# Cross attention and feed-forward: image units that make their weights once, turned by a trip through DRAM, and gate and up weights kept in DRAM

## The chip, the cores and the metric

The kernel runs on one core of one Trainium2 chip. The core has TensorE (matrix products; PE in the profile, with its weight loads as PEld), VectorE (DVE), ScalarE (ACT), GpSimd (POOL) and SyncE (SP), which here only issues transfers, and 16 DMA engines which all queues share. The metric is the device time of one execution in microseconds (us). Lower is better.

## The reference

Four batches of 1,024 tokens with 512 channels. Of each batch the first 768 tokens are image tokens, in three chunks of 256, and the last 256 are text.

```
q  = layernorm(x) @ Wq + bq                   # 16 heads of d = 32
k, v = ctx @ Wk + bk, ctx @ Wv + bv
s  = q k^T / sqrt(32), masked:                # an image query sees its own chunk of 256 keys
                                              # a text query sees 768 image keys and text keys up to its own
x  = x + softmax(s) v @ Wo + bo
y  = fake_quant(layernorm(x))                 # int8 steps, one scale for the whole tensor
h  = fake_quant(silu(y Wg^T) * (y Wu^T))      # 512 -> 1408, weights in int8 steps, one scale per row
x  = x + h Wd^T                               # 1408 -> 512
```

The softmax has to be that of the reference: the maximum of a row of scores is subtracted before the exponential. Only the kernel's inputs and this function count; how the weights of a softmax lie in memory on the way is free.

## The kernel before

**Units and steps.** The work of attention is cut into *blocks* of 256 queries (four per batch: three image blocks and the text block), a block into four groups of four heads, and a group into *parts*, the blocks of keys. An image block has one part (its own chunk), the text block four. One group and part is a *unit*: 256 queries, 256 keys, four heads. A batch has 12 image units and 16 text units, the whole attention 112; batches 0 to 2 are units 0 to 83, and batch 3 runs its first image block, then text, then the other two. One loop goes over the steps n, and step n holds pieces of several units:

- `maxima` of unit n: the scores with queries on partitions (TensorE, L446 image, L457 text; into two PSUM tiles of 128x1024, of which there are three pairs of banks for all scores), and from them on VectorE the negated maximum of each query (L450, L468). `minus_maxima` (L484, L485) splits it on GpSimd into two bf16 numbers in a tile nm2, and `shifts` (L492) has a DMA transpose turn that into rows, nmT.
- `weights` of unit n-5 (T_LAG): TensorE spreads the shift over the keys (L504), adds the scores *a second time*, now with keys on partitions (L509), and ScalarE takes the exponential into pT (L514, L518, 128x1024 each). GpSimd adds the two halves of keys into sp (L535).
- `values` of unit n-6 (V_LAG): TensorE multiplies pT by the values (L554) and, in the last part of a group, sums the weights with a matrix of ones (L573). ScalarE copies both out of PSUM (L964), VectorE takes the reciprocal of the sums (L588), and GpSimd multiplies (L589) into oT, from which the output product is made.

So an image unit computes its scores twice: the first for the maxima, the second the way round in which the value product needs the weights.

**What fills the rest.** Between these lie the projections of queries, keys and values and the output product (`column_groups`, L226: four products of 32 columns side by side), in "big" steps. `target(n)` says how many of them should be done by step n, `large(n)` takes one piece if the work is behind the target, and else an output. Projection results are taken by ScalarE (L295, L344), outputs by VectorE (L607), with the statistics of the second layer norm (L614 to L617). The inputs of a projection are loaded by `load_spread` (L142 to L146, four transfers of 128 KB on SP) and turned by a VectorE transpose in 32x32 blocks (`small_step`, L267). Behind the first batch's image units, `weight_unit` (L647 to L668) loads 128 rows of gate or up weights at a time, 22 in all, finds the scale on VectorE, rounds on ScalarE and GpSimd, and lets a DMA transpose (L668) put the result into wgT or wuT, which stay in SBUF until the feed-forward stage. Each block of x1_d, the residual in DRAM, is first filled with the bias (L883, SP's queue) and then gets x added (L885, GpSimd's queue).

**The order.** The program order is the order of issue on TensorE, VectorE, ScalarE and GpSimd; on SP, which carries most transfers, a scheduler sets it. An engine takes its instructions in order: one that waits holds all behind it.

**Feed-forward** starts after all attention: a reading of x1_d, rounding, gate and up products (`products`, L1116), SiLU (L1122), their product (L1143), rounding, and the down product (L1207, L1219).

## Time and profile before

| | us |
|---|---|
| median of the runs (three, 1126.51 to 1128.64) | 1127.62 |
| span of the profiled execution | 1126.9 |
| attention's first score product | 30.7 |
| batch 0: image units, text units | 97.3, 123.7 |
| batch 1: image units, text units | 90.5, 122.5 |
| batch 2: image units, text units | 89.1, 122.4 |
| batch 3 and the end of attention | 152.4 |
| feed-forward, from 828.6 | 298.3 |
| mean granted TensorE clock | 0.995 |
| moved by DMA: 135.87 MB, 121 GB/s over the span | |

A page of the profile gives the busy time of each engine over one execution, the span in 40 slices, the DMA queues, the chain of work that ended last (followed back from the last instruction), and groups of instructions: line, engine, operation, out<-in with partitions x elements, count, then busy time and the mean in ns of one, then the idle time of the engine just ahead of them and what ended it. Lines of a table by stage read: from and to, length, busy PE with its instructions, PEld, DVE, ACT, POOL, granted clock, mean DMA share, GB/s. In a list in order of time, a line is start, duration, engine, line, operation and count; successive instructions of one kind are drawn together.

In the fifth part of the page a reader finds the operations of `weights` and `values` of all 112 units: the second scores L509 with 113.8 us of TensorE, the exponentials L514 and L518 with 114.8 and 114.5 us of ScalarE, L535 with 189.3 and 140.2 us of GpSimd, the reciprocals L588 with 109.8 us of VectorE (63 of 1,743 ns).

### The profile page before, as it was taken

How to read it: one execution, taken by the hardware profiler on the slowest of the kernel's cores; microseconds unless marked ns; L12 is line 12 of the kernel's file. 1: busy time of each engine (PE TensorE's matmuls, PEld its weight loads, DVE VectorE, ACT ScalarE, POOL GpSimd, SP SyncE). 2: the span in 40 equal slices, each digit the busy share in tenths (PEclk: the TensorE clock that was granted, in tenths of full speed). 3: DMA queues.
4: the chain of work that ended last, by engine and by line, in shares of the span. 5: the costliest groups of instructions: out<-in, count | busy, mean ns of one | idle time of the engine just before them, and what ended most of it. 6: DMA issues, size and time to landing. Idle time of an engine off the chain costs nothing.

```text
span 1126.9 us, 31493 instructions
## 1 busy us (share of the span) xinstructions
PE 1106.6 (98%) x13829; PEld 553.9 (49%) x13851; DVE 783.9 (70%) x980; ACT 502.4 (45%) x701; POOL 532.0 (47%) x615
## 2 busy tenths in 40 slices
PE   9999999999999999999999999999999899998998
PEld 5545545454545444454545445555554344443344
DVE  2546677666576857666777657777667788877887
ACT  3234434353544334444434345545433465553553
POOL 1224546577755467775446467566752222110110
PEclk9999999999999999999999999999999899999999
DMA  7379645255744444332222113112321599310895
GB/s 234 101 219 284 114 96 127 61 113 98 121 62 115 93 105 78 101 81 63 59 84 80 48 60 83 47 51 63 114 67 58 179 295 255 70 38 23 302 386 194
DMA packets 138257, 135.87 MB, mean 121 GB/s; under 512 B 56060, under 2 KB 103432, under 8 KB 136712
## 3 DMA queue, kind: packets, MB, share of 16 engines
q1 hardware_dynamic: 115600, 91.91, 29.5%
q0 software_dynamic: 22208, 41.42, 14.3%
q8 instruction: 108, 1.77, 0.7%
q10 hardware_dynamic: 312, 0.53, 0.2%
q14 instruction: 29, 0.24, 0.1%
HBM read 79.96 MB, written 50.07 MB: 115 GB/s over the span
## 4 chain that ended last, share of the span: by engine, by line
PE 87%; POOL 4%; DVE 3%; ACT 2%; DMA 2%; issue 1%; SPq 0%; DVEq 0%; POOLq 0%; ACTq 0%
PE pv L226 10%; PE po L226 9%; PE av L554 9%; PE pp_q L226 8%; PE pp_kv L226 8%; PE t L509 7%; PE pg L1116 7%; PE pu L1116 7%; PE s L457 5%; PE pd L1219 5%; PE s L446 4%; POOL sp L535 3%; PE av L573 3%; PE t L504 3%; PE pd L1207 1%
## 5 line engine op out<-in xcount | busy, mean ns | idle before, releaser
L514 ACT ACTIVATE pT<-t 128x1024 f32<-128x1024 f32 x112 | 114.8, 1025 | 330.2 <-PE t L509 299.8
L535 POOL TENSOR_TENSOR sp<-sp,pT 128x1024 f32<-128x1024 f32 x84 | 189.3, 2254 | 43.2 <-ACT pT L518 39.8
L468 DVE TENSOR_REDUCE nmh<-s 128x2 f32<-128x1024 f32 (+1 forms) x128 | 145.2, 1157 | 61.2 <-PE s L457 59.0
L535 POOL TENSOR_TENSOR sp<-pT 128x1024 f32<-128x1024 f32 x59 | 140.2, 2375 | 95.7 <-ACT pT L518 87.3
L450 DVE TENSOR_REDUCE nmh<-s 128x4 f32<-128x1024 f32 x96 | 112.7, 1216 | 85.7 <-PE s L446 85.7
L226 PE MATMUL pp_q<-qT,Wq_sb 128*32 128x256 f32 x2048 | 121.3, 380 | 0.2
L226 PE MATMUL pv<-Wv_sb,kvT 128*32 128x512 f32 (+1 forms) x1088 | 120.5, 570 | 0.0
L554 PE MATMUL av<-pT,va 128*32 128x256 f32 (+1 forms) x1792 | 116.9, 377 | 0.0
L518 ACT ACTIVATE pT<-t 128x1024 f32<-128x1024 f32 x112 | 114.5, 1023 | 0.0
L509 PE MATMUL t<-qT,kT 32*128 32x256 f32 (+1 forms) x1792 | 113.8, 367 | 0.0
L226 PE MATMUL pp_kv<-kvT,Wk_sb 128*32 128x256 f32 x1920 | 112.5, 380 | 0.1
L226 PE MATMUL po<-Wo_sb,oT 128*32 128x512 f32 (+1 forms) x1120 | 112.1, 534 | 0.3
L588 DVE RECIPROCAL avs<-avs 128x256 f32<-128x256 f32 x63 | 109.8, 1743 | 0.0
L589 POOL TENSOR_TENSOR oT<-avs 128x256 f32<-128x256 f32 x63 | 48.0, 762 | 104.2 <-DVE avs L588 104.2
L509 PEld LDWEIGHTS t<-qT,kT 32*128 32x128 f32 x1792 | 88.3, 184 | 6.6
L1116 PE MATMUL pg<-xqT,wgT 128*128 128x512 bf16 x344 | 89.9, 381 | 1.1 <-DVE xqT L1077 0.5
L1116 PE MATMUL pu<-xqT,wuT 128*128 128x512 bf16 x345 | 89.8, 381 | 0.4
L1122 ACT ACTIVATE silu<-pg,sg 128x512 f32<-128x512 f32 x88 | 60.0, 686 | 64.9 <-PE pg L1116 62.8
L226 PEld LDWEIGHTS pp_q<-qT,Wq_sb 128*32 128x32 f32 x2048 | 63.3, 110 | 48.3 <-issue 5.8
L1143 DVE SCALAR_TENSOR_TENSOR h<-pu,su,silu 128x512 f32<-128x512 f32 x88 | 65.3, 746 | 30.3 <-PE pu L1116 27.6
L226 PEld LDWEIGHTS pp_kv<-kvT,Wk_sb 128*32 128x32 f32 x1920 | 60.2, 110 | 43.6 <-issue 2.3
L554 PEld LDWEIGHTS av<-pT,va 128*32 128x32 f32 x1792 | 47.0, 109 | 53.5 <-issue 30.3
(190 smaller groups left out, 1435.0 us busy)
## 6 DMA issues: line engine op xcount, KB each, us to landing
xt<-x_d SPq DMA_DIRECT2D x16, 1024.0 KB, 6.0
h<-h_d POOLq DMA_DIRECT2D x3, 2816.0 KB, 13.5
xb<-in_x_dram SPq DMA_DIRECT2D x16, 512.0 KB, 4.4
x_d<-bo_b SPq DMA_DIRECT2D x16, 512.0 KB, 5.7
x_d<-in_x_dram POOLq DMA_DIRECT2D x16, 512.0 KB, 7.6
xr<-x_d SPq DMA_DIRECT2D x16, 512.0 KB, 3.8
x_d<-xr POOLq DMA_DIRECT2D x16, 512.0 KB, 3.8
spread_kv<-in_ctx_dram SPq DMA_DIRECT2D x60, 128.0 KB, 3.0
```

What stands on the lines that cost most here:

```text
L226: nc.tensor.matmul(out[rows_of(j)], lhs[:, rows_of(j)], rhs, start=start, stop=stop, tile_position=(0, j * D), skip_group_check=True)
L450: nc.vector.tensor_reduce(nmh[:, h, :, :, 0], prs[h], AX.X, ALU.max, negate=True)
L468: nc.vector.tensor_reduce(nmh[:, h, :, i, half], s[:, :, :n], AX.X, ALU.max, negate=True)
L509: nc.tensor.matmul(prs[j // 2][:, j % 2, n, cols], kc[rows_of(j), g, n * P : (n + 1) * P], q[rows_of(j), g, cols], start=False, stop=(n == 1))
L514: nc.scalar.activation(pT[:, :2], prs[0], AF.Exp)
L518: nc.scalar.activation(pT[:, 2:], prs[1], AF.Exp)
L535: nc.gpsimd.tensor_tensor(sp[:, :, cols], a, pT[:, :, n, cols], ALU.add)
L554: nc.tensor.matmul(av[rows_of(j), 0, cols], va[:, n, g * P + j * D : g * P + (j + 1) * D], u.pT[:, j, n, cols], start=(u.part == 0 and n = ...
L588: nc.vector.reciprocal(avs[:, 1, :], avs[:, 1, :])
L1116: nc.tensor.matmul(ps, w[:, cc, ic * P : (ic + 1) * P], qT[:, cc, :], start=(cc == 0), stop=(cc == NCC - 1))
L1122: nc.scalar.activation(s, pg, AF.Silu, scale=sg[:, ic : ic + 1])
L1143: nc.vector.scalar_tensor_tensor(h[:, ic, :], pu, su[:, ic : ic + 1], s, ALU.mult, ALU.mult)
```

## The change

For the 36 image units of batches 0 to 2 (`u.rows`), the scores are made once, and the weights from them while queries are still on partitions:

- `exponents`: ScalarE reads the score tiles in PSUM, eight times 128x256 per unit, with the negated maximum as bias of each row, and sums each row as it goes (`accum_out`). The result is written in a blocked order (g n x k) into a tile E, a half unit (two heads) each; three buffers.
- `quotients`: VectorE takes the reciprocal of the 128x4 sums, GpSimd multiplies E by it (128x1024).
- `shuffle`: SP writes E to DRAM (512 KB; four buffers) and reads it back in four transfers of 128 KB into S (three buffers), so that blocks of 32 queries come to stand on the right partitions.
- `turned`: VectorE transposes S in 32x32 blocks into pT, keys on partitions.
- `row_values` at a lag of three steps (R_LAG): TensorE's value product, without the product for the sums; ScalarE copies the result straight into oT.

For these units `minus_maxima`, `shifts`, `weights` and `values` fall away. Inside a step the new pieces stand in this order: `maxima` of unit n, the `shuffle` of the second half of unit n-1, `turned` first half of unit n-2, `exponents` and `quotients` of the first half of unit n, the big step, the taking of its result, `exponents` of the second half, `turned` second half of unit n-2, the second `quotients`, the first half's `shuffle`; then what is left of text units in `weights` and `values`, and `row_values` of unit n-3. Batch 3 and all text units work as before.

Keys and values of image blocks are loaded with their rows in another order (`mixed`, eight transfers instead of four), to match the order of the keys in pT.

nmT has three buffers instead of five, nm2 three instead of four, and the gate and up weights no longer stay in SBUF beside these tiles: each transposed 128 rows go on to DRAM (`wq_d`, one more transfer on SP for each of 22), and `reload` brings both sets back (1.4 MB each) in batch 3, into the room of Wk, Wv and Wq, once the last projection and the last weight unit are done. The feed-forward products read them there.

The pacing changes too: in batches 1 to 3, `target` counts an image step in the first half of the image units three times, in the second half one and a half times, and a text step once; `large` no longer takes a piece ahead of the target in text steps; and an image step takes an output at its end if one waits and no other big step was taken there.

```diff
@@ -80,8 +80,7 @@
...
-    wgT = cpool.tile([P, NCC, FF], BF16, tag="wgT", name="wgT")
-    wuT = cpool.tile([P, NCC, FF], BF16, tag="wuT", name="wuT")
+    wq_d = {w: dram.tile([P, NIC, NCC * P], BF16, tag=f"wq_{w}_d", name=f"wq_{w}_d") for w in "gu"}
@@ -122,11 +121,13 @@
...
-        nmp = actx.enter_context(tc.tile_pool(name="nmp", bufs=5))
+        nmp = actx.enter_context(tc.tile_pool(name="nmp", bufs=3))
         qp = actx.enter_context(tc.tile_pool(name="qp", bufs=4))
         kp = actx.enter_context(tc.tile_pool(name="kp", bufs=7))
         ap = actx.enter_context(tc.tile_pool(name="ap", bufs=1))
-        wp = actx.enter_context(tc.tile_pool(name="wp", bufs=1))
+        bp = actx.enter_context(tc.tile_pool(name="bp", bufs=3))
+        wctx = ExitStack()
+        wp = wctx.enter_context(tc.tile_pool(name="wp", bufs=1, side="right"))
@@ -139,18 +140,29 @@
...
-        def load_spread(src, c):
...
             t = ld.tile([P, NQB * 2, P], F32, tag="cb", name=f"spread_{c}")
-            s = src.rearrange("(k q) (c m) -> c q k m", q=D, c=NCC)
             for i in range(NCC):
-                nc.sync.dma_start(t[i * D : (i + 1) * D], s[i])
+                to, cols = t[i * D : (i + 1) * D], slice(i * P, (i + 1) * P)
+                if not mixed:
+                    nc.sync.dma_start(to, src[:, cols].rearrange("(k q) m -> q k m", q=D))
+                    continue
+                for n in range(2):
+                    nc.sync.dma_start(to[:, n * 4 : (n + 1) * 4], src[:, cols].rearrange("(g n q) m -> n q g m", n=2, q=D)[n])
+            return t
...
@@ -441,6 +454,7 @@
...
             prs = [pair(f"s_{u.n}_{h}") for h in range(2)]
             if not k.text:
+                u.s, u.nmh = prs, nmh
@@ -467,6 +481,67 @@
...
+        def exponents(u, h):
+
+            e = bp.tile([P, 4, 2, 4, D], F32, tag="E", name=f"E_{u.n}_{h}")
+            sums = small.tile([P, 4], F32, tag="sums", name=f"sums_{u.n}_{h}", bufs=4)
+            for x in range(4):
+                jj, i = x // 2, x % 2
+                nc.scalar.activation(
+                    e[:, :, :, x, :].rearrange("p g n k -> p n g k"),
+                    u.s[h][:, jj, i, :].rearrange("p (n g k) -> p n g k", n=2, g=4),
+                    AF.Exp,
+                    bias=u.nmh[:, h, jj, i, 0:1],
+                    accum_out=sums[:, x : x + 1],
+                )
+            u.e[h], u.sums[h] = e, sums
+
+        def quotients(u, h):
+
+            nc.vector.reciprocal(u.sums[h], u.sums[h])
+            e = u.e[h].rearrange("p g n x k -> p (g n) x k")
+            nc.gpsimd.tensor_tensor(e, e, u.sums[h].unsqueeze(1).unsqueeze(3).to_broadcast([P, 8, 4, D]), ALU.mult)
+
+        def shuffle(u, h):
+
+            e = u.e.pop(h)
+            through = dram.tile([P, 4 * QB], F32, tag="e_d", name=f"e_d_{u.n}_{h}", bufs=4)
+            nc.sync.dma_start(through, e.rearrange("p g n x k -> p (g n x k)"))
+            u.spread[h] = t = bp.tile([P, 4, QB], F32, tag="S", name=f"S_{u.n}_{h}", bufs=3)
+            for g in range(4):
+                nc.sync.dma_start(t[g * D : (g + 1) * D], through.rearrange("(b q) (g f) -> g q b f", q=D, g=4)[g])
+
+        def turned(u, h):
+
+            if h == 0:
+                u.pT = wk2.tile([P, 4, 2, QB], F32, tag="pT", name=f"pT_{u.n}")
+            out = u.pT[:, 2 * h : 2 * h + 2].rearrange("p a b q -> p (a b q)").rearrange("p (y b k) -> p b y k", b=4, k=D)
+            nc.vector.transpose(out, u.spread.pop(h).rearrange("p b (y k) -> p b y k", k=D))
+
+        def row_values(u):
+
+            k, g = u.k, u.g
+            if "av" in state:
+                av = pair(f"av_{u.n}").rearrange("p a b q -> p (a b) q")[:, 0, :]
+            else:
+                av = ps_av.tile([P, 2, QB], F32, tag="av", name=f"av_{u.n}")[:, 0, :]
+            va = V[k.c]
+            pT = u.pT.rearrange("p a b q -> p (a b q)").rearrange("p (h n j q) -> p h n j q", h=2, n=2, j=2)
+            for n in range(2):
+                for j in range(4):
+                    nc.tensor.matmul(
+                        av[rows_of(j)],
+                        va[:, n, g * P + j * D : g * P + (j + 1) * D],
+                        pT[:, j // 2, n, j % 2, :],
+                        start=(n == 0),
+                        stop=(n == 1),
+                        tile_position=(0, j * D),
+                        skip_group_check=True,
+                    )
+            if g == 0:
+                k.begin()
+            return av
+
@@ -665,11 +742,13 @@
...
             def transpose():
-                nc.sync.dma_start_transpose(dst[:, :, ic * P : (ic + 1) * P], q)
+                t = wk2.tile([P, NCC, P], BF16, tag="wqT", name=f"wqT_{what}_{ic}", bufs=1)
+                nc.sync.dma_start_transpose(t, q)
+                nc.sync.dma_start(wq_d[what][:, ic, :], t.rearrange("p c f -> p (c f)"))
...
 
-        T_LAG, V_LAG = 5, 6
+        T_LAG, V_LAG, R_LAG = 5, 6, 3
@@ -680,6 +759,8 @@
...
+        for u in units[:LATE]:
+            u.rows, u.e, u.sums, u.spread = not u.k.text, {}, {}, {}
@@ -768,7 +849,9 @@
             first, n = 6 * BIG, n + 1.5
             if n < n_img:
                 return first + (NQB - 1) * first * n / n_img
-            return NQB * first * (1 + (n - n_img) / (n_img + n_text))
+            whole, n = divmod(n - n_img, n_img + n_text)
+            done = min(n, n_text) + 3 * min(max(n - n_text, 0), n_img / 2) + 1.5 * max(n - n_text - n_img / 2, 0)
+            return NQB * first * (1 + whole + done / (n_text + 4.5 * n_img / 2))
@@ -800,7 +883,7 @@
...
-                elif can_big(n) and spent < target(n) + 3 * BIG:
+                elif can_big(n) and spent < target(n) + (0 if units[n].k.text else 3 * BIG):
@@ -830,6 +913,15 @@
...
+        wT = {}
+
+        def reload(w):
+            if not wT:
+                wctx.close()
+                fw = ctx.enter_context(tc.tile_pool(name="fw", bufs=1, side="right"))
+                for x in "gu":
+                    wT[x] = fw.tile([P, NIC, NCC, P], BF16, tag=f"w{x}T", name=f"w{x}T")
+            nc.sync.dma_start(wT[w].rearrange("p i c f -> p i (c f)"), wq_d[w])
@@ -870,8 +962,14 @@
...
-                if u.part == u.parts - 1:
+                if u.part == u.parts - 1 and not u.rows:
                     minus_maxima(u)
+            now = u if n < len(units) and u.rows else None
+            before = units[n - 2] if 2 <= n < len(units) + 2 and units[n - 2].rows else None
+            if previous is not None and previous.rows:
+                shuffle(previous, 1)
+            if before is not None:
+                turned(before, 0)
@@ -889,7 +987,16 @@
...
+            if now is not None:
+                exponents(now, 0)
+                quotients(now, 0)
             full = large(n)
+            if now is not None or before is not None:
+                complete()
+            if now is not None:
+                exponents(now, 1)
+            if before is not None:
+                turned(before, 1)
@@ -901,19 +1008,22 @@
...
+            if now is not None:
+                quotients(now, 1)
+                shuffle(now, 0)
...
             def weights_now():
-                if T_LAG <= n < len(units) + T_LAG:
+                if T_LAG <= n < len(units) + T_LAG and not units[n - T_LAG].rows:
...
             def values_now(between=lambda: None):
-                if n < V_LAG:
+                if n < V_LAG or units[n - V_LAG].rows:
@@ -940,6 +1050,14 @@
...
+            r = units[n - R_LAG] if R_LAG <= n < len(units) + R_LAG else None
+            rav = None
+            if r is not None and r.rows:
+                need_values(r.k.c, n)
+                if r.g == 0:
+                    while len(outputs) >= OUTS:
+                        step_output()
+                rav = row_values(r)
@@ -958,12 +1076,22 @@
...
                 early[0] = False
+            elif now is not None and outputs:
+                step_output()
...
+            if rav is not None:
+                nc.scalar.copy(r.k.oT[:, r.g, :], rav)
+                if r.g == NCC - 1:
+                    later.append(lambda k=r.k: finished(k))
+            if at_big == len(jobs) and n_weights == 2 * NIC and not weight_stages and not any(b.__name__ in ("largest", "quantise") for b in background) and not late_rest and not wT and n >= LATE:
+                reload("g")
+            elif wT and len(wT) == 2 and "done" not in state:
+                state["done"] = reload("u")
+            if n >= V_LAG and not units[n - V_LAG].rows:
@@ -1113,11 +1241,11 @@
...
         def products(ps, w, ic, qT):
             for cc in range(NCC):
-                nc.tensor.matmul(ps, w[:, cc, ic * P : (ic + 1) * P], qT[:, cc, :], start=(cc == 0), stop=(cc == NCC - 1))
+                nc.tensor.matmul(ps, w[:, ic, cc, :], qT[:, cc, :], start=(cc == 0), stop=(cc == NCC - 1))
...
```

## The prediction

> **What bounds the kernel now.** I read the page's busy line and its chain first, then a table by stage whose borders are the first score matmuls of each stage, then one step in order of time.
>
> ```profile
> PE 1106.6 (98%) x13829; PEld 553.9 (49%) x13851; DVE 783.9 (70%) x980; ACT 502.4 (45%) x701; POOL 532.0 (47%) x615
> ...
> PE 87%; POOL 4%; DVE 3%; ACT 2%; DMA 2%; issue 1%; SPq 0%; DVEq 0%; POOLq 0%; ACTq 0%
> ```
> TensorE is the bound: 87% of the chain, nobody else above 4%. The stages (length, then busy PE, PEld, DVE, ACT, POOL, clock, DMA share, GB/s) are batch 0's image units, its text units, the same for batches 1 and 2, and batch 3:
>
> ```profile
> 30.70:128.00 97.30, 96.29 (x1450) 49.32 (x1446) 56.64 (x60) 36.48 (x66) 31.20 (x60) 1.00 0.77 199
> 128.00:251.70 123.70, 122.45 (x1830) 61.57 (x1826) 86.76 (x108) 52.78 (x79) 76.02 (x73) 1.00 0.44 97
> 251.70:342.20 90.50, 88.64 (x1301) 43.56 (x1297) 56.61 (x59) 39.31 (x57) 65.03 (x79) 1.00 0.57 94
> 342.20:464.70 122.50, 122.05 (x1830) 61.41 (x1827) 88.68 (x112) 51.64 (x76) 72.09 (x65) 1.00 0.45 100
> 464.70:553.80 89.10, 88.65 (x1303) 43.58 (x1299) 56.58 (x59) 39.20 (x57) 59.32 (x74) 1.00 0.26 72
> 553.80:676.20 122.40, 121.95 (x1764) 59.31 (x1760) 85.08 (x107) 49.60 (x71) 64.35 (x53) 1.00 0.22 66
> 676.20:828.60 152.40, 152.23 (x2521) 89.21 (x2517) 109.80 (x140) 75.23 (x100) 104.39 (x103) 1.00 0.25 71
> ```
> VectorE has 34 us to spare in an image stage of 90, and DMA is at 57% in batch 1. One image step by its TensorE starts:
>
> ```profile
> 302.37 1.15 PE L446 MATMUL s<-kT,qT 32*128 32x256 f32 x16
> 303.44 2.78 PE L226 MATMUL po<-Wo_sb,oT 128*32 128x512 f32 x24
> 306.16 0.40 PE L504 MATMUL t<-nmT,onesb 2*128 2x512 bf16 x4
> 307.35 1.07 PE L554 MATMUL av<-pT,va 128*32 128x256 f32 x16
> ```
> Start to start: scores 1.07, first three quarters of an output or projection step 2.72 (so 3.6 whole), shifts and second scores 1.19, values 0.89 by the next start at 308.24; the sums of the weights (L573) take 0.45 to 0.55.
>
> The rows for what is added:
>
> ```profile
> L267 DVE STREAM_TRANSPOSE kvT<-spread_kv 128x1024 f32<-128x1024 f32 x15 | 32.0, 2135 | 24.4 <-PE pv L226 23.4 <-PE pp_q L226 0.9
> L450 DVE TENSOR_REDUCE nmh<-s 128x4 f32<-128x1024 f32 x96 | 112.7, 1216 | 85.7 <-PE s L446 85.7
> L588 DVE RECIPROCAL avs<-avs 128x256 f32<-128x256 f32 x63 | 109.8, 1743 | 0.0
> L295 ACT ACTIVATE qT<-pp_q,bqk 128x256 f32<-128x256 f32 x64 | 27.5, 471 | 46.6 <-PE pp_q L226 46.6
> ```
>
> **The change, part by part.** *TensorE, removed.* 36 image units lose L504, L509 and L573: 36 x (1.19 + 0.45) = 59 us. Nothing is added on TensorE. That is the most it can gain. Walking the built order with these costs gives 100.6 us of TensorE work in the image stages of batches 1 and 2 (87.4 before) and 87.6 in the text stages (120.6 before): the new pacing moves projections into image steps. Some 10.8 us of it goes into batch 3, which becomes 152.4 + 10.8 = 163.2. Before, such sums stand 2% under the measured stages, so I multiply by 1.02.
>
> *VectorE.* Each image unit loses one reciprocal (1.74) and gains two small ones (0.17 each, from the 128x1 row at 164 ns) and two transposes of 128x1024. A transpose lies between 1.22 (any other VectorE row on 1,024 elements, L450) and 2.13 (L267). L267 reads every fourth element (its source is rearranged as "e c"); the new one reads runs of 32 neighbours, so I take 1.3, the row nearest in its access, and keep 2.13. It was a choice: by operation L267 is nearer.
> [...] No row here has an unstrided transpose.
>
> Where it matters: from the sixth image step of batch 1 to the second text step (nine steps) the order holds for VectorE 20 us of score maxima, 0.9 mask, 18 transposes, 2.4 reciprocals, 13 output statistics, 1.7 input statistics, 4.1 output adds, 6.4 projection transposes, 1.7 old reciprocal. With 2.13 that is 90 us, with 1.3 it is 75; TensorE has 65.4. So VectorE is the longest engine there in either case.
>
> *ScalarE.* Eight 128x256 exponentials replace two of 128x1024: 0.37 to 0.47 each (a pair of L295 takes 0.84), up to 0.67 if the sum is read out by an extra instruction (nearest small row 204 ns). With 0.5: 4.0 for 2.05, plus a copy of 0.37 for 0.59. Hidden under steps of 9 us; in the first five image steps two text exponentials come on top, about 9 in all.
>
> *GpSimd.* Two multiplications of 2.38 (L535's row) for one add, one oT product (0.76) and two nm copies (0.46): 4.8 for 3.6. In the five image steps that still carry text weights it holds 5 x (4.8 + 4.5) + 4 = 50 us against TensorE's 46; I take 52.
>
> *The round trip.* A half-unit is written (512 KB) and read back in four 128 KB pieces. Rows: 512 KB lands in 3.1 to 4.7 us in the quiet stage, issue 0.4; four spread issues take 1.8, the last lands 2.9 later. Walk, from a step's scores: maxima to 2.4, exponentials to 4.6, product to 7.5, write landed 11.9, reads issued 13.7. The second half's product ends near 10.5 but its write is behind those reads on SP: issued 13.7 to 15.3 past a spread or a load, landed 19. Its E buffer is wanted two steps later, 2T + 2.5, so T is at least 8.3; SP itself needs 8 to 9 us of each step. The design just closes at steps of 8.7 to 9.5. Each 512 KB through the queues costs some 3 us of all 16 engines (4 KB packets 0.17, 1 KB 0.047), 70 us per image stage, beside 23 (batch 2) to 51 (batch 1). The landing of the same transfer in those two stages:
>
> ```profile
> x_d<-xr POOLq DMA_DIRECT2D x2, 512.0 KB, 6.7
> x_d<-xr POOLq DMA_DIRECT2D x2, 512.0 KB, 3.6
> ```
> First the loaded stage, then the quiet one. I add 0.5 us on 24 steps, 12 us, for batches 0 and 1.
>
> *FFN weights.* 22 more writes of 128 KB on SP, each waiting for its transpose (landing 2.6 to 2.8): mostly in text steps, where SP has gaps, so nothing on the path; with no cover it is 22 x 2.7 = 59 on SP, part of case D. Two reloads of 1.4 MB (5.8 to 7.3 by the h_d rows) are issued some 10 steps before attention ends; the attention tail hides them. FFN itself is unchanged. Three instead of five nmT buffers make SP wait one step in batch 3's image units, where a shift is wanted three steps later: nothing. Kv loads in mixed order and 8 issues instead of 4 cost 1.8 on SP each.
>
> **Sum, case A.** Batch 0: four filling steps 28, ten steps 88 (TensorE 81.1 x 1.02, some round trip), fourteen text steps 76.7 x 1.02 = 78: 194 for 221. Batches 1 and 2: 52 + 78 (nine steps at 8.7, VectorE 75) + 75 x 1.02 = 76.5, 206.5 each for 213 and 211.5. Batch 3: 163.2 for 152.4. In all 770 for 797.9, -28; with the loaded DMA -16. The span of 1126.9 becomes 1111; the median of the runs is 0.7 above the span, so 1112.
>
> **The rivals.**
> - *B, slower: VectorE's transposes cost 2.13.* The nine steps become 90, batch 0's ten 96: 202 + 2 x 218.5 + 163.2 = 802, +4, with DMA +16: 1144; in-order waits of 1 us on 28 steps could make it 1171. For it: the only transposing row there is. It decides from about 1.7 us a transpose, where the sum is zero. The page would show DVE above 90% in image stages and TensorE waiting for psum pairs.
> - *C: everything hides.* Then the 59 us come off whole: 1068. For it: the chain has little but TensorE; against it: VectorE's 75 against 65.
> - *D, slower: the round trip is late.* With landings of 6.5 and 4.2, as in batch 1 now, the walk closes only at T = 11; 28 steps x 2 in place of the 12: 1155. For it: DMA at 70 + 51 us in 118; against: halves can lag a step.
> - *Cancelled:* a transpose near 1.7 leaves it within 0.2%, which is about what a measurement of this kernel can tell from no change.
>
> **How the numbers follow.** A 0.36 (1095 to 1125), C 0.13, B 0.28, D 0.18, cancelled 0.05. Faster is A and C, 0.49; slower B and D, 0.46. The likeliest is A, 1112; the range that leaves out a tenth at each end reaches from between A and C, 1076, to 1160.
>
> **What would show it.** Right: transposes of S at 1.2 to 1.4, image stages of 110 to 120 us, text stages near 90, no L504/L509 in image units, batch 3 some 11 longer. Wrong: transposes at 2.1 (B); exponentials or SP waiting on DMA landings of e_d with image steps of 11 (D); a granted clock under 1.00 in image stages, since TensorE pauses there for the first time (the clock now falls to 0.5 for 6.8 us after the pause at 875 to 881).

## The result: 10% slower, with TensorE waiting where it never waited

The changed kernel takes 1245.82 us (median of four runs, 1240.08 to 1249.74) against 1128.13 before, a ratio of 1.104 (95% interval 1.101 to 1.107). The page of the profiled execution (span 1248.0), its busy line and its chain of waits:

```profile
PE 1117.0 (89%) x12875; PEld 540.3 (43%) x12875; DVE 815.2 (65%) x1087; ACT 558.6 (45%) x1207; POOL 539.7 (43%) x542
...
PE 56%; DMA 15%; DVE 9%; SPq 7%; POOL 6%; issue 4%; ACT 3%; DVEq 0%; POOLq 0%; ACTq 0%
```

TensorE fell from 87% of the chain to 56%, and DMA and SP's queue, 2% together before, are now 22%. The same table by stage as before the change (borders at the first score product of each stage, image and text units in turn, then batch 3; columns as there):

```profile
31.80:163.00 131.20, 107.37 (x1408) 49.02 (x1405) 77.74 (x105) 68.49 (x250) 54.05 (x50) 0.91 0.89 256
163.00:282.20 119.20, 104.11 (x1312) 49.93 (x1308) 74.00 (x101) 34.95 (x52) 56.12 (x55) 0.90 0.71 184
282.20:416.20 134.00, 112.13 (x1484) 51.94 (x1480) 81.82 (x106) 74.60 (x249) 82.88 (x63) 0.92 0.85 229
416.20:535.90 119.70, 103.90 (x1312) 49.47 (x1308) 73.91 (x101) 35.56 (x53) 56.99 (x57) 0.90 0.56 129
535.90:662.20 126.30, 109.00 (x1484) 51.23 (x1480) 81.73 (x106) 74.02 (x248) 77.23 (x59) 0.95 0.76 224
662.20:781.70 119.50, 103.80 (x1313) 49.44 (x1309) 73.90 (x101) 35.56 (x53) 50.28 (x52) 0.90 0.41 125
781.70:948.70 167.00, 163.14 (x2712) 94.53 (x2708) 108.42 (x132) 77.26 (x106) 102.38 (x100) 1.00 0.25 69
```

Image stages grew by 34, 44 and 37, text stages lost 3 to 5, batch 3 grew by 15; the rest of the program moved by 2. Of the five engines none but TensorE is above 65% in the image stages; the DMA engines are at 0.89, 0.85 and 0.76 there (0.77, 0.57 and 0.26 before). The granted clock, 1.00 in every stage before, is 0.90 to 0.95 wherever the change works.

Where the 119 us of attention went can be put as a sum of three numbers, an accounting taken from the trace from the first score product of unit 0 to that of unit 111: the time in which TensorE had nothing running; the time that it was busy with the clock granted at half, which I price at half its length (the first 24 products of an output step took 5.35 within a spell, at 358.16 in the change, and 2.78 at full clock, at 303.44 before); and what remains, length less idle time less half of that, the work at full clock.

| | length | idle | busy at half clock | work at full clock |
|---|---|---|---|---|
| before | 797.9 | 5.6 | 0 | 792.3 |
| the change | 916.9 | 113.4 | 100.0 | 753.5 |
| without the trip (e1) | 821.7 | 55.4 | 34.4 | 749.2 |
| the change, old pacing (e6) | 882.6 | 94.2 | 81.2 | 747.9 |
| without the trip, old pacing (e5) | 792.7 | 38.0 | 23.5 | 742.9 |
| half bytes, six S, one more step of lag (e13) | 818.2 | 55.1 | 41.1 | 742.6 |

The change took 39 us of work off TensorE. It then left TensorE idle for 108 us more, in 28 pauses of over 1 us where there was one, and behind the pauses it worked for 100 us at half clock, by that price another 50. -39 + 108 + 50 = 119.

What TensorE waited for in attention, the five longest (total, times, longest):

```profile
PE s L460 <- ACT E L490: 21.9, 11, 6.9
PE po L238 <- DVE xr L684: 17.6, 4, 6.3
PE av L650 <- POOL sp L610: 11.9, 7, 3.2
PE pp_kv L238 <- DVE xr L684: 10.7, 1, 10.7
PE po L238 <- ACT kT L307: 9.8, 2, 5.2
```

The first scores of a unit wait for PSUM tiles that ScalarE's exponentials have to empty; the exponentials wait 61.0 for VectorE's maxima, and VectorE holds, in order between its maxima, the transposes, which wait 45.8 for S.

One such pause in order of time, first TensorE, then VectorE, then SP's queue (start, duration, engine, line; what ended the idle time before it in brackets):

```profile
412.58 3.64 PE L238 MATMUL po<-Wo_sb,oT 128*32 128x512 f32 x32 [2.23 <-ACT qT L307]
416.15 1.15 PE L471 MATMUL s<-kT,qT 32*128 32x256 f32 x16
423.64 6.02 PE L238 MATMUL po<-Wo_sb,oT 128*32 128x512 f32 x32 [6.34 <-DVE xr L684]
```
```profile
422.89 0.69 DVE L684 TENSOR_TENSOR xr<-po,xr 128x512 f32<-128x512 f32 x1 [8.26 <-DMA xr<-x_d]
423.50 2.35 DVE L482 TENSOR_REDUCE nmh<-s 128x2 f32<-128x1024 f32 x2
425.76 1.24 DVE L519 STREAM_TRANSPOSE pT<-S 128x1024 f32<-128x1024 f32 x1
```
```profile
405.90 5.16 SPq L509 DMA_DIRECT2D e_d<-E  x2
411.16 1.45 SPq L397 DMA_DIRECT2D xn_d<-xb  x1
412.71 4.05 SPq L512 DMA_DIRECT2D S<-e_d  x8
416.87 0.38 SPq L137 DMA_DIRECT2D xr<-x_d  x1
```

SP issues two writes of E, eight reads of S, and only then the residual block xr, which has nothing to do with the trip. It lands 6 us later, VectorE waits 8.26 for it, TensorE 6.34 for the PSUM bank that VectorE has to empty, and the same 32 products that took 3.64 at 412.58 take 6.02 at 423.64, at half clock.

### The profile page after: what moved, and what is told of

Same layout as the page of the kernel before. It is cut to its first block, busy times and chain, and to the rows that moved or that the text cites. A ratio compares the mean times of both kernels' runs of the same rounds, so it can differ in the third digit from the quotient of the medians.

```text
span 1248.0 us, 30791 instructions
## 1 busy us (share of the span) xinstructions
PE 1117.0 (89%) x12875; PEld 540.3 (43%) x12875; DVE 815.2 (65%) x1087; ACT 558.6 (45%) x1207; POOL 539.7 (43%) x542
## 4 chain that ended last, share of the span: by engine, by line
PE 56%; DMA 15%; DVE 9%; SPq 7%; POOL 6%; issue 4%; ACT 3%; DVEq 0%; POOLq 0%; ACTq 0%
PE pv L238 6%; DMA S<-e_d 6%; PE pg L1244 6%; PE po L238 6%; PE pu L1244 6%; SPq L512 5%; PE s L471 5%; PE av L631 4%; PE t L584 4%; DMA e_d<-E 4%; PE pp_q L238 4%; PE pp_kv L238 4%; POOL sp L610 3%; PE pd L1347 2%; POOL E L503 2%
## 5 line engine op out<-in xcount | busy, mean ns | idle before, releaser
L503 POOL TENSOR_TENSOR E<-E,sums 128x1024 f32<-128x1024 f32 x72 | 136.6, 1909 | 160.9 <-DVE sums L501 119.5
L610 POOL TENSOR_TENSOR sp<-sp,pT 128x1024 f32<-128x1024 f32 x84 | 188.4, 2243 | 40.9 <-ACT pT L593 37.6
L490 ACT ACTIVATE E<-s,nmh 128x256 f32<-128x256 f32 x288 | 133.2, 484 | 116.7 <-DVE nmh L464 61.0
L589 ACT ACTIVATE pT<-t 128x1024 f32<-128x1024 f32 x76 | 78.1, 1027 | 202.7 <-PE t L584 195.2
L238 PE MATMUL po<-Wo_sb,oT 128*32 128x512 f32 (+1 forms) x1088 | 123.8, 598 | 34.9 <-DVE xr L684 17.6
L519 DVE STREAM_TRANSPOSE pT<-S 128x1024 f32<-128x1024 f32 x72 | 88.8, 1236 | 62.5 <-DMA S<-e_d 45.8
L471 PE MATMUL s<-kT,qT 32*128 32x256 f32 (+1 forms) x1024 | 90.0, 413 | 9.6 <-DVE nmh L482 6.3
L460 PE MATMUL s<-kT,qT 32*128 32x256 f32 x768 | 67.1, 421 | 22.7 <-ACT E L490 21.9
L631 PE MATMUL av<-pT,va 128*32 128x256 f32 (+1 forms) x1216 | 80.6, 374 | 6.2 <-POOL pT L598 5.2
L238 PEld LDWEIGHTS po<-Wo_sb,oT 128*32 128x32 f32 x1088 | 34.1, 117 | 107.1 <-issue 58.8
L584 PE MATMUL t<-qT,kT 32*128 32x256 f32 (+1 forms) x1216 | 80.3, 374 | 0.0
```

Of the source, the lines that this page charges most:

```text
L238: nc.tensor.matmul(out[rows_of(j)], lhs[:, rows_of(j)], rhs, start=start, stop=stop, tile_position=(0, j * D), skip_group_check=True)
L471: nc.tensor.matmul(prs[j // 2][:, j % 2, kk, :w], q[rows_of(j), g, i * P : (i + 1) * P], K[k.keys[2 * half + kk]][rows_of(j), g, :w], star ...
L490: nc.scalar.activation(e[:, :, :, x, :].rearrange("p g n k -> p n g k"), u.s[h][:, jj, i, :].rearrange("p (n g k) -> p n g k", n=2, g=4), ...
L503: nc.gpsimd.tensor_tensor(e, e, u.sums[h].unsqueeze(1).unsqueeze(3).to_broadcast([P, 8, 4, D]), ALU.mult)
L519: nc.vector.transpose(out, u.spread.pop(h).rearrange("p b (y k) -> p b y k", k=D))
L584: nc.tensor.matmul(prs[j // 2][:, j % 2, n, cols], kc[rows_of(j), g, n * P : (n + 1) * P], q[rows_of(j), g, cols], start=False, stop=(n == 1))
```

## The experiments

### The trip, the pacing, and what is left without them

e1 lets VectorE turn E itself; e5 does so with the old pacing; e6 is the whole change with the old pacing; e4 keeps the old units everywhere.

```diff
-            nc.sync.dma_start(through, e.rearrange("p g n x k -> p (g n x k)"))
...
+            u.spread[h] = e.rearrange("p g n x k -> p g (n x k)")      # e1, e5; E bufs=6
```
```diff
-            whole, n = divmod(n - n_img, n_img + n_text)
...
+            return NQB * first * (1 + (n - n_img) / (n_img + n_text))   # e5, e6
-                elif can_big(n) and spent < target(n) + (0 if units[n].k.text else 3 * BIG):
+                elif can_big(n) and spent < target(n) + 3 * BIG:
```
```diff
-            u.rows, u.e, u.sums, u.spread = not u.k.text, {}, {}, {}
+            u.rows, u.e, u.sums, u.spread = False, {}, {}, {}           # e4
```

> The changed kernel without the trip through DRAM: VectorE turns E itself (six E buffers, no S), so the blocks of 32 do not change partitions and the values are those of wrong queries; every instruction on the four engines is still there. Theory T (the trip is late; engines' work is not the matter): 1075 to 1110, image stages of 105 to 115 where the changed kernel has 131 to 139. Theory E (the image steps are held by the engines' own order: VectorE, exponents ahead of the taking of a projection): above 1180, little better than the changed kernel's 1246.

> The changed kernel with the old units everywhere (u.rows False): what is left of the change is the gate and up weights through DRAM, the pacing, three nmT and nm2 buffers, mixed loading. If these cost little, 1120 to 1145; if the pacing or the weights' trip is a good part of the loss, 1160 or more.

> The kernel without the trip (VectorE turns E, the same part left out) with the pacing of the kernel before (its target and large). Theory P (the new pacing costs: 14.7 in batch 3, and TensorE pauses in text steps where it waits for GpSimd, each followed by a spell at half clock): the 1152 of the run without the trip fall to 1085 to 1115. If the image steps themselves hold it whatever the pacing, 1135 or more.

> The whole change with the pacing of the kernel before. Theory P alone: the same 35 to 65 fall off as without the trip, 1180 to 1210. Rival: with less TensorE work in image steps the trip, which sets their length, only shows more, and TensorE pauses more often: 1235 to 1260.

Measured: e1 1152.09 (ratio 1.021), e4 1143.13 (1.013), e5 1130.43 (1.004), e6 1215.52 (1.078). So the trip costs 94 with the new pacing (1245.82 - 1152.09) and 85 with the old (1215.52 - 1130.43), and the pacing 22 to 30. All three of e1, e5 and e6 came out between the two ranges that were given for them: the lower one (T, then P) missed by 42, 15 and 5, and the upper one asked for 28, 5 and 20 more. The trip is most of the loss, as T has it, and something is left that T does not name, since even without the trip the kernel is no faster than before. e4's 15 lie in batch 3 alone, whose span is 166.8 there, 166.7 in the whole change and 152.1 before: the pacing keeps back projections that batch 3 then has to do (2,712 products there in the change, 2,521 before). With the old pacing (e6) batch 3 takes 152.4 by the borders of the table above, as before the change.

In e1 the image steps go as the prediction summed them. Batch 1 by its first score products, in the prediction's three parts: five image steps, the nine to the second text step, and fourteen text steps:

```profile
245.89:299.00 53.11, 48.73 (x753) 25.55 (x749) 30.31 (x37) 38.59 (x112) 45.73 (x34) 1.00 0.39 82
299.00:371.75 72.75, 66.02 (x893) 29.37 (x889) 61.16 (x81) 37.02 (x140) 39.71 (x33) 1.00 0.41 96
371.75:466.96 95.21, 87.71 (x1152) 43.17 (x1149) 63.56 (x90) 34.53 (x51) 54.41 (x54) 0.93 0.46 100
```

53.1 for 52, 72.8 for 78, but 95.2 for 76.5. What TensorE waited for in e1's attention, largest first (total, times, longest):

```profile
PE av L646 <- POOL sp L606: 11.5, 7, 3.2
PE pp_kv L238 <- DVE xr L680: 6.1, 1, 6.1
PE s L460 <- ACT E L490: 5.5, 7, 1.4
PE av L627 <- POOL pT L594: 5.2, 3, 1.7
```

With the projections moved out of the text steps, TensorE catches up with GpSimd's sums and masks (POOL above) there and pauses, and a spell at half clock of 10.2 to 13.7 follows in each batch. With the old pacing (e5) the text stages of batches 1 and 2 are at clock 1.00.

### Is it VectorE?

e12 takes E as it lies, without trip and transposes.

```diff
-            nc.vector.transpose(out, u.spread.pop(h).rearrange("p b (y k) -> p b y k", k=D))
...
+                        flat[j // 2][:, 4 * n + 2 * (j % 2) : 4 * n + 2 * (j % 2) + 2, :],   # E itself; R_LAG = 2
```

> Old pacing, no trip and no transposes: TensorE's value products take E as it lies, one step earlier, so queries and keys are mixed up; 72 x 1.24 = 89 of VectorE's work are gone, nothing else. If VectorE's work sets the image steps that remain at 9.0 to 9.7 (run without a trip: 1130): 1075 to 1100. If it is another engine's order or latency: 1115 or more.

Measured 1110.74 (0.984 [0.978, 0.990]), 20 faster than e5 though 89 us of VectorE's work are gone, and between the two ranges that were given. VectorE matters somewhat, but it is not what sets most of these steps. By first maxima, steps 31 to 34 of attention in batch 1 take 9.7 to 11.7 each in e5 and 9.3 to 9.4 in e12; steps 35 to 37 take 8.6 to 9.1 in both, and the work of TensorE in such a step (two pieces of 3.6, scores 1.1, values 0.9) is 9.2.

### Which property of the trip?

> As the run without the trip, but E is still written to DRAM and read back into an S that nobody uses: all transfers are there and only an E buffer (five of them) can be late. Same part left out. If the load on the 16 DMA engines slows everything else (theory D: volume), it stays at 1190 or more. If only the waiting for S costs (theory Q: the order of SP's queue and its latency), it lies within 25 us of the run without the trip, 1080 to 1130.

```diff
+            u.spread[h] = e.rearrange("p g n x k -> p g (n x k)")      # E bufs=5
-            u.spread[h] = t = bp.tile([P, 4, QB], F32, tag="S", name=f"S_{u.n}_{h}", bufs=3)
+            t = bp.tile([P, 4, QB], F32, tag="S", name=f"S_{u.n}_{h}", bufs=1)
```

Measured 1248.02. It does not tell theory Q from D: with one S buffer each read had to wait for the read before it (98 us of SP's waits), so the run made a new queue of its own.

> The writes of E are issued on ScalarE's queue, at the places where the kernel has them; SP keeps only the reads. Theory Q: in SP's queue as the scheduler set it three writes stand ahead of twelve reads, so a read waits for writes of later halves whose products are not made yet; with writes gone from it image steps fall from 11.5 to 9 or 10, and the time to 1130 to 1170. Theory D (volume, DMA 80 to 93% busy in image steps): the same bytes, so 1220 or more.

```diff
-            nc.sync.dma_start(through, e.rearrange("p g n x k -> p (g n x k)"))
+            nc.scalar.dma_start(through, e.rearrange("p g n x k -> p (g n x k)"))
```

> The whole change, but the residual block xr (512 KB, L137) is loaded on ScalarE's queue instead of SP's, where it stood behind eight reads of S. TensorE waited 17.6 + 10.7 for VectorE's add of xr, with half-clock spells after them. Theory (loads queued behind the trip are a main cost): 1205 to 1225. If the trip itself paces the steps, 1240 or more.

```diff
-                    self.xr = load_block(x1_d, self.k.c, "xr", bufs=2)
+                    self.xr = load_block(x1_d, self.k.c, "xr", bufs=2, queue=nc.scalar)
```

Measured 1261.03 for e3 and 1253.20 for e8, both slower than the change. A single kind of transfer moved to another queue did not help; theory Q as I had put it, by the order of writes and reads on SP, falls. e3 meets D's number, but what the volume alone is worth shows only in e11 below. In e3 a write goes out as soon as its product is ready, yet from the exponentials of a half unit to its transpose it takes 24 to 26, as in the change (24 to 25). Most of that span is the two steps of lag: without any trip (e1) it is 18 to 20. In e8 VectorE's wait for xr fell from 24.3 to 11.1, but its waits for S and for the block xb rose from 69 to 97 together, so the place of xr on SP's queue alone is not what to cure.

> The pacing of before, and only every second image unit of batches 0 to 2 (18 of 36) makes its weights once; the others work as before. A half unit's trip then has a step of its own. If the trip was late because four transfers of 512 KB a step are too many for SP and the queues, it now hides, and 18 x 1.64 = 30 less TensorE work shows in part: 1100 to 1125. If the wait is one of latency (turned two steps later), the same waits come in half the steps: 1150 or more.

```diff
-            u.rows, u.e, u.sums, u.spread = not u.k.text, {}, {}, {}
+            u.rows, u.e, u.sums, u.spread = not u.k.text and u.g % 2 == 0, {}, {}, {}   # and old pacing
```

Measured 1198.24 (1.061). Half the units, half the traffic, and still 70 slower than before: relief of the queues by halving the load is not enough, which speaks for latency. The transposes wait 50.3 for S in all, as in e6 (48.5), though there are half as many. How much of the 70 is the trip is not shown, since this mixture was not run without it; TensorE's three longest waits there are for GpSimd and ScalarE (13.7, 11.3 and 11.1).

> The whole change with the old pacing, and every turned and row_values one step later (units n-3 and n-4). In the old-pacing run a second half's trip took 14 to 16 from the end of its product to S, and VectorE turned it 2 on average after it was there. Theory L (the trip's latency against two steps of lag is the loss): 1215 falls to 1140 to 1165, image steps near the 9.0 to 9.7 of the run without a trip. Theory B (throughput of SP, of three E and three S buffers, of the queues): 1195 or more.

> As the run with one more step of lag, with the writes of E on ScalarE's queue, so that reads and writes do not stand in one queue. Theory L: no gain over the other, within 15. If SP's single queue is what is left, 20 or more faster than the other, down to 1130.

```diff
-        T_LAG, V_LAG, R_LAG = 5, 6, 3
+        T_LAG, V_LAG, R_LAG = 5, 6, 4
-            before = units[n - 2] if 2 <= n < len(units) + 2 and units[n - 2].rows else None
+            before = units[n - 3] if 3 <= n < len(units) + 3 and units[n - 3].rows else None   # old pacing; e10 also e3's line
```

Measured 1255.65 (e9) and 1237.56 (e10): 40 and 22 slower than e6, where theory L had promised 50 to 75 faster. e10 is 18 faster than e9, between the two answers that were given for it. The waits say why. First e6 (two steps of lag), then e9 (three), what VectorE's transposes and ScalarE's exponentials waited for in attention:

```profile
DVE pT L519 <- DMA S<-e_d: 48.5, 18, 5.0
...
ACT E L490 <- DMA e_d<-E: 22.3, 6, 7.3
```
```profile
ACT E L490 <- DMA e_d<-E: 95.1, 19, 10.6
...
DVE pT L519 <- DMA S<-e_d: 11.2, 5, 2.6
```

The extra step did what it was made for, 48.5 became 11.2. But S was then held a step longer, with three buffers, and SP's reads stood waiting for VectorE to free one, with the writes that free E behind them:

```profile
SPq L512 <- DVE sums L501: 65.0, 17, 9.9
SPq L512 <- DMA e_d<-E: 57.9, 32, 4.5
...
SPq L512 <- DVE pT L519: 21.6, 11, 4.1
```

The first row names sums, the small reciprocal that stands behind a transpose on VectorE. By the times of the trace it is the transpose that frees S: in 28 of 69 half units the first read starts 0.03 after the end of the transpose three half units earlier, which had the same buffer.

To have six S buffers in the same room, the next runs make the transfers half as wide: the same number of them, S tiles of half the size. Only half of each tile then makes the trip, and VectorE turns that half twice.

```diff
-            nc.sync.dma_start(through, e.rearrange("p g n x k -> p (g n x k)"))
+            nc.sync.dma_start(through[:, : 2 * QB], e[:, :2].rearrange("p g n x k -> p (g n x k)"))
-            u.spread[h] = t = bp.tile([P, 4, QB], F32, tag="S", name=f"S_{u.n}_{h}", bufs=3)
+            u.spread[h] = t = bp.tile([P, 4, P], F32, tag="S", name=f"S_{u.n}_{h}", bufs=3)   # 6 in e13, e17, e18
```

> Old pacing, two steps of lag, every transfer of the trip half as wide (256 KB and four of 64 KB a half unit; as many transfers and packets; VectorE turns the half that arrived twice, so half of the weights are wrong). Volume as the cause: the trip's 85 (1215 against 1130) fall to about half, 1165 to 1180. Latency and issue: 1195 or more.

> As the run with half the bytes (two steps of lag, 1196), with six S buffers instead of three: the control for the run with one more step of lag and six buffers (1148). If the lag is what brought the 48, it stays at 1185 to 1205; if the buffers did, it is at 1160 or less.

> Old pacing, transfers of the trip half as wide (wrong values as before), and now six S buffers of half the size, turned and row_values one step later. With three S buffers the extra step made it 40 slower, since the reads waited for S. If latency against the lag is the cause, and the buffers only hid it, 1196 falls to 1135 to 1160. If E (three buffers) and SP's one queue set the pace, 1185 or more.

> As the run with one more step of lag, half the bytes and six S buffers (1148), with the writes on ScalarE's queue. If SP's one queue is the rest between 1148 and the 1130 without a trip: 1130 to 1140. If not, within 8 of 1148 or slower, since ScalarE now waits for GpSimd's products.

| old pacing | lag 2 | lag 3 |
|---|---|---|
| full width, three S buffers | 1215.52 (e6) | 1255.65 (e9) |
| half the bytes, three S buffers | 1196.35 (e11) | |
| half the bytes, six S buffers | 1182.23 (e17) | 1147.74 (e13) |
| no trip | 1130.43 (e5) | |

Half the bytes are worth 19, not the 35 to 50 that volume as the cause asked for; three more S buffers are worth 14, and with both in place the extra step of lag 34. In e13 the transposes wait 3.1 for S in all, and 17.0 more for something that the profile does not name. e17 came out 3 under its range, so part of the 48 that I put to the lag is the buffers'. The 17 between e13 and e5 stay open: e18, which writes from ScalarE's queue, took 1178.74, 31 slower than e13, so relief of SP's queue in this way does not bring them, but the run made waits of its own. In e18 ScalarE waits 16.7 for GpSimd's product ahead of its exponentials into pT (text units), and TensorE 18.1 for those exponentials (2.9 in e13); that this is the cause of the 31 is argued from these two waits, not tested.

> Old pacing, two steps of lag, full width, but S is read in one transfer of 512 KB with rows as they were written, instead of four of 128 KB (blocks of 32 are not exchanged, so the values are those of wrong queries). SP issues 2 instead of 5 for a half unit, the packets are of 4 KB instead of 1 KB. If SP's issues and small packets are the cost: 1215 falls to 1165 to 1185. If the waits on landings are: 1200 or more.

> As the run with one read, and the writes of E on ScalarE's queue: SP has one instruction for each half unit. If SP as a serial resource is the cause, 1145 to 1165; if the two landings in a row are (write 4 to 5, read 3 to 4), within 15 of the run with one read.

```diff
-            for g in range(4):
-                nc.sync.dma_start(t[g * D : (g + 1) * D], through.rearrange("(b q) (g f) -> g q b f", q=D, g=4)[g])
+            nc.sync.dma_start(t.rearrange("p b f -> p (b f)"), through)   # e15 also e3's line
```

Measured 1208.16 and 1197.29: two instructions instead of five on SP, and rows read in pieces of 4 KB instead of 1 KB, give 7, the second queue 11 more, both as the theory of landings had it. By these 7, SP's time for issuing is a small part.

Taken together: with two steps of lag and three buffers a half unit's trip is late, VectorE waits for S with the residual adds and maxima queued behind it, and TensorE behind those. No cure by itself brings more than 19 of the 85 (e11), and in e9 one sees the wait move to the next buffer; only less traffic, more buffers and more lag together (e13) come near a free trip. Full width with more buffers was not run, so whether the bytes are needed for that is open.

### The half clock, tested on the kernel before

> The kernel before with idle bf16 products on TensorE in its two pauses behind attention: six more at 877 (pause of 1.50), three more behind the scale of x, thirteen ahead of the scale of h (pause of 3.24). Theory: a pause is what brings the half clock (6.8 at 880, 3.4 at 1044); without pauses both spells go, and 3 to 5 us with them: 1123 to 1125. Rival: the spells come from something else, and it stays at 1128 or is 1 slower.

```diff
-        for _ in range(12):
+        for _ in range(18):            # idle_tail
...
-    for _ in range(4):
+    for _ in range(7):                 # idle_x
...
+    for _ in range(13):                # idle_h0, ahead of tensor_scale(hmax, "h", ps_x)
+        nc.tensor.matmul(idle.rearrange("p (a b) -> p a b", a=4), identb, identb.unsqueeze(1).to_broadcast([P, 4, P]), start=True, stop=True)
```

The two stretches with a pause, of the kernel before and then of e16 (length, then busy times, the granted clock third from the end):

```profile
876.00:890.00 14.00, 10.56 (x48) 4.88 (x47) 8.32 (x23) 5.99 (x9) 3.99 (x9) 0.76 0.54 174
1038.00:1050.00 12.00, 7.85 (x30) 3.04 (x29) 10.24 (x18) 5.69 (x7) 0.00 (x0) 0.86 0.81 300
```
```profile
876.00:890.00 14.00, 12.04 (x64) 5.56 (x64) 9.36 (x23) 7.78 (x12) 4.15 (x7) 1.00 0.57 183
1038.00:1050.00 12.00, 10.49 (x47) 4.38 (x47) 9.48 (x17) 8.19 (x8) 0.00 (x0) 1.00 0.92 344
```

With the pauses filled both spells are gone, 0.76 and 0.86 became 1.00. The time is 1125.29 against 1127.48 in the same rounds, ratio 0.998 [0.997, 0.999]: about half of what I expected, outside its range by 0.3, but clear of the noise, and the only kernel here that leaves nothing of the reference out and is faster than before. The two spells hold 8.2 of busy time at half clock, which the accounting above would price at 4.1; for these two stretches it is too high.

## Why the prediction was wrong

The miss of 134 is two terms of the sum. Without the trip the new kernel takes 1152 (e1) where case A without its 12 for the trip says 1100: 52. The trip itself took 94 where the sum has 12: 82. The 52 lie in the text steps: the fourteen of each batch were summed as 231 in three batches and took 284 in e1, while the image steps and batch 3 of e1 agree with the sum within 6 in every part.

- **The sum on TensorE was too large, and not the cause.** "36 x (1.19 + 0.45) = 59 us": by the table above 39 came off in the change, and 43 to 50 in e1, e5, e6 and e13. Ten to twenty of it were mis-sized; the miss is 134.
- **The price of VectorE's transposes held.** The value taken was 1.3 against 2.13; measured 1.24 (72 of them, 1,204 to 1,247 ns):

```profile
L519 DVE STREAM_TRANSPOSE pT<-S 128x1024 f32<-128x1024 f32 x72 | 88.8, 1236 | 62.5 <-DMA S<-e_d 45.8 <-POOL sp L610 9.3 <-issue 4.0
L279 DVE STREAM_TRANSPOSE kvT<-spread_kv 128x1024 f32<-128x1024 f32 x15 | 31.9, 2124 | 22.7 <-DMA xb<-in_x_dram 11.7 <-PE pv L238 8.7 <-PE pp_q L238 2.3
```

  L279, which reads every fourth element, stays at 2.12; the transpose of S, which reads neighbours, is 1.24. Both write runs of 32 neighbours, so the reading is what tells them apart; that it sets the price was my estimate, and a run that changes it alone was not made. So rival B was rightly put behind, and case A's nine steps of 78 are 72.8 without the trip. That VectorE was the bound of those steps is not shown, e12 speaks against it.
- **The step that failed is the walk of the round trip**, "The design just closes at steps of 8.7 to 9.5", and its price, "I add 0.5 us on 24 steps, 12 us". It cost 85 to 94. The walk followed the second half's write only to the deadline of its E buffer, not on through its own reads to the transpose. With the walk's own numbers (write landed 19, reads issued in 2, landed in 3 more) S is there at 24, when the transpose of step n+2 is wanted at about 2T + 5, by my estimate (2T + 6.0 in e1, median): T of 9.5 and nothing to spare for any late landing. Measured in the change, the second half's product ends 13.9 after its scores (median; the walk has 10.5, e1 has 11.0), S lands 15.3 after that (mean), and its transpose stands 10.4 behind the scores of its step instead of 6.0. Lateness feeds on itself here: a late transpose holds the maxima behind it on VectorE, and so the next products.
- **Rival D had the mechanism** ("the round trip is late", steps of 11), and the image steps are 11 (134.0 / 12 in batch 1). It was given 0.18 and 1155. Its 28 x 2 = 56 for the first fourteen steps of the batches stand against 72 measured, half clock included. The rest of its miss of 91 is mainly the text steps, which took 302 in the change where the sum has 231: 71.
- **A pause was given no price beyond its length.** The prediction named a granted clock under 1.00 as a sign, and had a spell of 6.8 at half clock before its eyes, but no term of the sum and no rival carried it. By the accounting it is 50 of the 119.
- **The text steps**, "fourteen text steps 76.7 x 1.02 = 78", were summed as TensorE's work alone. The pacing left TensorE without filler there, so it pauses, mostly for GpSimd: the fourteen take 95.2 in batch 1 even without the trip, at clock 0.93, 16 to 19 more than forecast in each of three batches (94.5, 95.2, 94.7). In batch 1 that is 82.5 of work at full clock (the sum has 75 x 1.02 = 76.5), 7.5 of pauses (4.8 of them for GpSimd's sums and masks) and 5 for the half clock. With the old pacing and no trip (e5) they take 91.0 in batch 1 although they hold more of the projections, at clock 1.00.
- **Batch 3** was put at 163.2 and took 167.0; moved work is most of it, as forecast.
- **SP's queue** was walked in the order of the program; the order that the scheduler set has two or three writes ahead of their reads in 25 of 37 groups, and other loads behind. Its part is small by itself: moving the writes (e3) or the xr load (e8) off it did not help, and fewer issues on it brought 7 (e14).

## What to carry to other kernels

This kernel, bound by an engine at 98%, paid for new waits (108 us of pauses), not for new work (39 us came off that engine): before taking work off such an engine, follow each half of the new path to its last reader, with the landings of the loaded stage, and count the buffers that stand on it at that lag. By the table above, with its price of the half clock, the new pauses of TensorE cost 1.3 to 1.5 times their length with the spells that followed them, so a pause is to be priced with its spell. And the trip on SP's busy queue stood ahead of loads that belong to quite other parts, as the xr load shows (VectorE waited 8.26 for it); here, moving that load alone did not pay (e8).

## What the runs showed of the hardware that I had not expected

- In this case's traces the clock is granted at half in spells of 3.4 to 23.9, multiples of 3.41 (over all runs 121 of one, 108 of two, 34, 13 and 4 of three, four and five, and one of seven; those that a trace's end cuts off are left out). I counted the pauses of TensorE of 0.5 or more over all runs that had no other such pause within 3.5 on either side. A spell began in the pause or within 3.5 of its end for 1 of 164 of 0.5 to 1 us, 23 of 88 of 1 to 2, 40 of 66 of 2 to 3, 69 of 74 of 3 to 5, and all 54 that were longer. So pauses shorter than the shortest spell, 3.41, came with one in a quarter of the cases from 1 to 2 and in most from 2 to 3. In e16 the first spell went with the filling of a pause of 1.50, which one of 0.38 had followed.
- In e16 idle products of TensorE in the two pauses took both spells away whole (granted clock 0.76 and 0.86 before, 1.00 in both stretches then), at no cost that the times show, 1125.29 against 1127.48.
- GpSimd's multiplication of 128x1024 by four broadcast columns took 1.91 (L503, 72 of them), the sum of two tiles of this size 2.37 (L610, 97); the prediction had taken 2.38 for both.
